# Where the banks of turned attention weights stand between the projections of the next batch

## The chip, the cores and the metric

The kernel runs on one core of one Trainium2 chip. The metric is the device time of one launch in microseconds (us), as the median of several runs. The kernel before takes 2846.47 us (median of three runs, 2845.55 to 2849.2).

## What is computed

The reference is a two-layer block on x of 16 batches x 100 rows x 512 channels, with a context of 16 x 722 x 384, all in fp32. Each layer adds a gated cross-attention to x and then a gated feed-forward network (a mixture of experts in layer 0, a quantized network in layer 1):

```
q = LN(x) @ Wq (+ bq);  k = ctx @ Wk (+ bk);  v = ctx @ Wv (+ bv)
p = softmax(q k^T * D**-0.5)            # over 722 keys, per head
x = x + tanh(g) * ((p v) @ Wo + bo)     # layer 0: 16 heads of 32, layer 1: 8 heads of 64, no bq, bk, bv
x = x + tanh(g_ffn) * ffn(LN(x))
```

The change is in the attention that both layers share.

## The kernel before

**Steps.** The attention goes by 64 steps, (b, m): a batch b and a block m of 128 channels, which holds G = 4 heads in layer 0 and G = 2 in layer 1. TensorE's instructions run in the order in which the program writes them (`manual_schedule` for PE); the other engines' order is set when the program is built, each by a plan of when its operands will be ready, and each then works through its list in that order. `run` (L489 on) writes the order. In the step for (b, m) it issues

- `scores` of the next step (L369): eight short matmuls into two tiles of two PSUM banks each (pool `s`, two tiles). VectorE copies each head's scores out, negated, with a running minimum (L379 and L392; L402 joins the two halves in layer 0) into one of four `ns` tiles. In layer 0 a call covers half of the keys, so a step has two calls; in layer 1 one call covers all;
- `attend` of the step before (L458): 24 products in layer 0 and 12 in layer 1 (two matmul records each) of values and turned weights, chunk by chunk of 128 keys; L465 (VectorE) multiplies the result by the reciprocal of the sums and writes it to `tT`;
- `turn` of this step: ScalarE's exponentials (`softmax`, L411) lie as 100 rows x 722 keys per head, and attend needs keys on partitions. For each pair of heads there are twelve transpositions (L434) into three PSUM banks of four, which ScalarE (L447) or VectorE (L449) copies to a tile `pT`; which of the two is set by whether m + pair + bank is odd. The last bank of the last pair has a fifth transposition (L442) of the reciprocals `rinv`, which VectorE makes with L429 from the sums that the exponentials leave;
- `softmax` of the next step: one exponential per head.

**Units.** Between these stand units of other work, one call each: a bank of the next batch's keys (`keys`, L207, six matmul records, copied by ScalarE at L219 or L221) or values (`values`, L232 and L239), a bank of queries (L329 and L338), of the output projection (`project`, L476 and L483), of a turned tile of x (L131 and L132), of router logits (L627 and L630), or work without TensorE such as moments. Keys and values come at 3.5 units per step, the rest at steps given by hand; the two lists are joined to `units`, the second kind first.

**Banks.** All of these but `scores` take their PSUM bank from one pool of four (tag "mm"), in order; a claim waits until the copy out of the bank that was claimed four claims before has ended. `pT` has three buffers.

**The cut.** With two pairs per step (layer 0), of n units (2n+4)//5 go ahead of pair 0's three banks, up to (3n+4)//5 behind them, then the second call of scores, pair 1's three banks, and the rest. With one pair (layer 1), (n+1)//2 units stand ahead of the three banks and the rest behind.

Of the kernel before, what the change touches and what calls it, by code (L numbers as in the profile page):

```python
# [8 lines left out]
F32 = mybir.dt.float32  # L9
# [7 lines left out]
P = 128  # L17
B, T, C = 16, 100, 512
# [7 lines left out]
NS = -(-S // P)  # L26
# [23 lines left out]
def bcast(ap, *shape):  # L50
    return ap.to_broadcast(list(shape))
# [6 lines left out]
def tiles_for(b):  # L58

    return [i for i in range(NTT) if (i * P + rows_of(i) - 1) // T == b]  # L60
# [74 lines left out]
class Attention:  # L135
# [281 lines left out]
                accum_out=self.sums[b][:, h : h + 1],  # L417
            )

    def turn(self, b, m, pair):  # L420


        nc, D, G = self.net.nc, self.D, self.G
        last = pair == G // 2 - 1
        t = self.p3.tile([P, 2 * NS + 1, T], F32, tag="pT", name="pT")
        if last:
            rinv = self.p2.tile([T, G, D], F32, tag="rinv", name="rinv")
            sums = self.sums[b][:, m * G : (m + 1) * G]
            nc.vector.reciprocal(rinv, bcast(sums.unsqueeze(2), T, G, D))  # L429
        for q in range(3):  # L430
            ps = self.ps_m.tile([P, 5, T], F32, tag="mm", name="ps_t")
            for i in range(4):
                j, c = divmod(4 * q + i, NS)
                nc.tensor.transpose(  # L434
                    ps[:, i, :],
                    self.prob(b, m * G + 2 * pair + j)[:, c * P : (c + 1) * P],
                    self.net.ident[:T, :T],
                )
            n = 4
            if last and q == 2:  # L440
                n = 5
                nc.tensor.transpose(  # L442
                    ps[:, 4, :], rinv.rearrange("p g d -> p (g d)"), self.net.ident[:T, :T]
                )
            to = t[:, 4 * q : 4 * q + n, :]
            if (m + pair + q) % 2:
                nc.scalar.copy(to, ps[:, :n, :])  # L447
            else:
                nc.vector.tensor_copy(to, ps[:, :n, :])  # L449
        self.pT[b, m, pair] = t  # L450

    def attend(self, b, m):
        nc, D, G = self.net.nc, self.D, self.G
# [35 lines left out]
    def run(self, given, after_project=None, more=()):  # L489

        parts = 2 if self.G == 4 else 1
        steps = [(b, m) for b in range(B) for m in range(KC)]
        last_tile = lambda g: ((g + 1) * GT - 1) // P
        extra = {i: [] for i in range(len(steps) + 40)}
        for at, *unit in more:
            extra[at].append(tuple(unit))
        for g in range(1, B // GB):
            at = 4 * KC * (g - 1)  # L500
            for n, i in enumerate(range(last_tile(g - 1) + 1, last_tile(g) + 1)):
                extra[at + 2 + n].append((self.query_input, i))
            for m in range(KC):
                extra[at + 7 + 2 * m].append((self.queries, g, m))
        for b in range(B):
            for i in tiles_for(b):
                at = (b + 1) * KC + 1
                extra[at].append((self.project, i))
                for later, *unit in after_project(i) if after_project else ():
                    extra[at + later].append(tuple(unit))  # L510
        todo = [u for b in range(1, B) for u in self.keys_and_values(b)]
        for i, (b, m) in enumerate(steps):
            if m == 0 and b + 2 < B and b + 2 not in self.cxs:
                self.load_ctx(b + 2)

            upto = max(0, min(len(todo), int(3.5 * (i + 1) - 2)))
            units = extra[i] + todo[given:upto]
            given = max(given, upto)
            nxt = steps[i + 1] if i + 1 < len(steps) else None
            if nxt:  # L520
                self.scores(*nxt, 0)
            if i:
                self.attend(*steps[i - 1])
            n = len(units)
            cut = [0, (n + 1) // 2, n] if parts == 1 else [0, (2 * n + 4) // 5, (3 * n + 4) // 5, n]
            for f, *a in units[cut[0] : cut[1]]:
                f(*a)
            self.turn(b, m, 0)
            for f, *a in units[cut[1] : cut[2]]:
                f(*a)  # L530
            if parts == 2:
                if nxt:
                    self.scores(*nxt, 1)
                self.turn(b, m, 1)
                for f, *a in units[cut[2] :]:
                    f(*a)
            if nxt:
                self.softmax(*nxt)
        self.attend(*steps[-1])
        for i in range(len(steps), len(steps) + 40):  # L540
            for f, *a in extra[i]:
                f(*a)
# [390 lines left out]
def quantized_ffn(net, p, gate, out):  # L933
# [3 lines left out]
    with ExitStack() as ctx:  # L937
# [129 lines left out]
        with tc.manual_schedule(engines={PE}):  # L1067
            for k in range(KC):
                turn(0, FG[0], k)
            for i in range(1, F1 // FT):  # L1070
                weights(i)
            for g, tiles in enumerate(FG):
                between = {}
                if g + 1 < len(FG):
                    normal(FG[g + 1])
                    for k in range(KC):
                        between[NF - 6 + k] = [(turn, g + 1, FG[g + 1], k)]
                feed(g, tiles, between)
# [486 lines left out]
```

## Time and profile before

| what | before |
|---|---|
| median of three runs | 2846.47 us |
| profiled execution, its time | 2848.7 us |
| its span | 2847.0 us |
| granted clock, mean | 0.99 |
| stretch 60 to 930 us, layer 0's attention: TensorE / VectorE / ScalarE busy | 863.8 / 438.8 / 431.0 us |
| stretch 1000 to 1650 us, most of the experts: TensorE busy | 644.2 us |
| stretch 1760 to 2460 us, layer 1's attention: TensorE / VectorE / ScalarE busy | 697.6 / 240.6 / 249.2 us |

The profile is of one execution; its span is the time from the first to the last instruction, and its time is that of the launch. A row of the timeline names the start, the length, the engine, the line of the kernel, the operation, what it writes and reads with the buffer numbers left out, how many records are merged, and, in brackets, how long the engine had been idle and what ended that. PE is TensorE's matmul, PEld its load of weights, DVE is VectorE, ACT is ScalarE, POOL is GpSimd. A matmul's end is modelled and longer than the distance to the next matmul, so lateness on TensorE is read from the distance between starts.

### The profile page before, as it was taken

The numbers are of one execution on the slowest core, as the hardware profiler recorded it, in microseconds if no ns is written. First come the engines' busy times: TensorE is split into PE (matmuls) and PEld (weight loads), VectorE is DVE, ScalarE is ACT, GpSimd is POOL, SyncE is SP. The second block draws the span as 40 slices with busy tenths as digits, with TensorE's granted clock in tenths as the row PEclk, the third lists the DMA queues.
The fourth block names the chain that finished last, engine by engine and source line by source line (L and its number), as shares of the span: only waits on it lengthen the run. The fifth ranks groups of instructions, "written<-read, shape, count | busy, mean of one in ns | idle before, by whom it ended". The sixth has DMA issues, their size and how long they took to land. (4 is left out here: it accounts for less than half of the span.)

```text
span 2847.0 us, 41099 instructions
## 1 busy us (share of the span) xinstructions
PE 2790.3 (98%) x17360; PEld 1732.7 (61%) x17360; DVE 934.0 (33%) x2441; ACT 872.2 (31%) x1726; POOL 168.6 (6%) x187
## 2 busy tenths in 40 slices
PE   8999999999999999999999989999999999799999
PEld 4555555555555678878878845555565555444554
DVE  3544544454455500000000073333333333521100
ACT  2544554454455310000000034333333334211110
POOL 2000000000000000000000050000000000301000
PEclk9999999999999999999999999999999999899999
DMA  4000100000000389898988541000000000430000
GB/s 160 17 17 17 33 24 24 17 28 33 17 24 5 117 329 336 318 318 313 321 313 311 186 130 36 17 16 32 16 17 32 17 32 1 141 96 15 11 12 9
DMA packets 129877, 278.04 MB, mean 98 GB/s; under 512 B 5825, under 2 KB 5841, under 8 KB 129169
## 3 DMA queue, kind: packets, MB, share of 16 engines
q1 hardware_dynamic: 117888, 246.80, 24.9%
q0 software_dynamic: 5088, 16.28, 1.6%
q10 hardware_dynamic: 6704, 12.19, 1.1%
q8 instruction: 141, 2.31, 0.3%
q14 instruction: 56, 0.45, 0.0%
HBM read 260.31 MB, written 14.94 MB: 97 GB/s over the span
## 5 line engine op out<-in xcount | busy, mean ns | idle before, releaser
L232 PE MATMUL ps_v<-wv_a,ctx_a 128*128 128x512 f32 (+1 forms) x1152 | 523.3, 598 | 4.0 <-ACTq L898 1.6
L207 PE MATMUL ps_k<-ctx_a,wk_a 128*128 128x361 f32 x1488 | 488.1, 472 | 0.0
L840 PE MATMUL ps_h<-xT,w 128*128 128x128 f32 x3712 | 421.1, 276 | 4.0 <-DVEq L1450 4.0
L840 PEld LDWEIGHTS ps_h<-xT,w 128*128 128x128 f32 x3712 | 418.6, 193 | 4.7 <-issue 4.7
L207 PEld LDWEIGHTS ps_k<-ctx_a,wk_a 128*128 128x128 f32 x1488 | 271.7, 190 | 150.2 <-issue 12.8
L232 PEld LDWEIGHTS ps_v<-wv_a,ctx_a 128*128 128x128 f32 (+1 forms) x1152 | 204.2, 185 | 238.5 <-issue 227.9
L392 DVE TENSOR_SCALAR_CACHE_REDUCE ns<-ps_s 100x361 f32<-100x361 f32 x512 | 244.5, 525 | 206.8 <-PE ps_s L369 184.9
L434 PEld LDWEIGHTS ps_t<-ident,pr_a 100*128 100x128 f32 x2304 | 215.7, 142 | 83.3 <-issue 43.8
L411 ACT ACTIVATE pr_a<-ns,extremes 100x722 f32<-100x722 f32 x256 | 227.1, 889 | 67.8 <-DVE extremes L402 67.7
L434 PE MATMUL ps_t<-ident,pr_a 100*128 100x100 f32 x2304 | 239.3, 253 | 4.4 <-DVE tT_a L465 4.2
L449 DVE COPY pT<-ps_t 128x400 f32<-128x400 f32 (+1 forms) x288 | 169.6, 593 | 193.4 <-PE ps_t L434 185.5
L369 PE MATMUL ps_s<-kT_a,qT_a 32*100 32x361 f32 (+1 forms) x1536 | 213.9, 502 | 7.4 <-DVE ns L379 4.9
L239 ACT COPY v_a<-ps_v 128x512 f32<-128x512 f32 x192 | 111.3, 579 | 340.1 <-PE ps_v L232 340.1
L860 PE MATMUL ps_o<-w,midT 128*128 128x512 f32 x464 | 203.9, 592 | 0.0
L379 DVE TENSOR_SCALAR_CACHE_REDUCE ns<-ps_s 100x722 f32<-100x722 f32 x128 | 111.3, 907 | 276.1 <-PE ps_s L369 276.1
L447 ACT COPY pT<-ps_t 128x400 f32<-128x400 f32 (+1 forms) x288 | 146.8, 511 | 170.1 <-PE ps_t L434 152.4
L1047 PE MATMUL ps_z<-ffn_w,y_ffn 128*128 128x512 f32 (+1 forms) x416 | 190.8, 594 | 0.0
L1029 PE MATMUL ps_y<-hT,ffn_w 128*128 128x384 f32 (+2 forms) x512 | 183.9, 503 | 0.2 <-DVE hT L1012 0.2
L429 DVE RECIPROCAL rinv<-sums_a 100x128 f32<-100x128 f32 x128 | 121.8, 951 | 184.7 <-ACT pr_a L411 184.7
L458 PEld LDWEIGHTS ps_pv<-pT,v_a 128*32 128x32 f32 (+3 forms) x4608 | 135.2, 120 | 69.0 <-issue 45.8
L851 DVE TENSOR_TENSOR midT<-silu,ps_h 128x512 f32<-128x512 f32 x58 | 39.9, 687 | 389.1 <-PE ps_h L840 389.1
L458 PE MATMUL ps_pv<-pT,v_a 128*32 128x100 f32 (+3 forms) x4608 | 163.1, 254 | 1.1 <-DVE pT L449 0.6
(160 smaller groups left out, 1803.1 us busy)
## 6 DMA issues: line engine op xcount, KB each, us to landing
w<-in_L_ffn_w SPq DMA_DIRECT2D x116, 1024.0 KB, 7.2
w<-in_L_ffn_wo SPq DMA_DIRECT2D x29, 2048.0 KB, 10.2
ctx_a<-in_ctxT SPq DMA_DIRECT2D x30, 1083.0 KB, 5.2
q<-in_L_ffn_fc_q SPq DMA_DIRECT2D x8, 1024.0 KB, 5.3
ffn_w<-in_L_ffn_fc_scales SPq DMA_DIRECT2D x8, 1024.0 KB, 10.8
rows<-ot ACTq DMA_DIRECT2D x29, 256.0 KB, 8.0
xn_d<-xn_moe ACTq DMA_DIRECT2D x12, 256.0 KB, 2.0
ctx_a<-in_ctxT SPq DMA_DIRECT2D x6, 361.0 KB, 5.5
```

What stands on the lines that cost most here:

```text
L207: nc.tensor.matmul(ps, self.wk[:, k, m * P : (m + 1) * P], self.cxs[b][:, k, c * SH : (c + 1) * SH], start=(k == 0), stop=(k == KK - 1),)
L232: nc.tensor.matmul(ps[:n], self.cxs[b][:, k, c * P : c * P + n], self.wv[:, k, :], start=(k == 0), stop=(k == KK - 1),)
L369: nc.tensor.matmul(pss[n // 2][:, n % 2, :SH], self.qT[g][j * D : (j + 1) * D, m, q], self.kT[b, m][j * D : (j + 1) * D, c * SH : (c + 1) ...
L392: nc.vector.tensor_scalar(self.negated[b, m][j][:, part * SH : (part + 1) * SH], pss[j // 2][:, j % 2, :SH], -1.0, BIG, ALU.mult, ALU.min, ...
L411: nc.scalar.activation(self.prob(b, h)[:, :S], ns, AF.Exp, bias=self.nmax[b][:, h : h + 1], scale=-1.0, accum_out=self.sums[b][:, h : h + 1],)
L434: nc.tensor.transpose(ps[:, i, :], self.prob(b, m * G + 2 * pair + j)[:, c * P : (c + 1) * P], self.net.ident[:T, :T],)
L449: nc.vector.tensor_copy(to, ps[:, :n, :])
L458: nc.tensor.matmul(ps[j * D : (j + 1) * D, :], self.v[b][:n, c, m * P + j * D : m * P + (j + 1) * D], self.pT[b, m, j // 2][:n, j % 2 * NS ...
L840: nc.tensor.matmul(ph[:, f, :], w[:, n, k, f * P : (f + 1) * P], self.xT[j][:, k, :], start=(k == 0), stop=(k == KC - 1),)
L860: nc.tensor.matmul(po, self.midT[j, f // 4][:, f % 4, :], w[:, f, :], start=(f == 0), stop=(f == KF - 1),)
L1029: nc.tensor.matmul(ps[:, :nt], w1[f // nf][:, k, f % nf * P : (f % nf + 1) * P], hT[g][:, k, :nt], start=(k == 0), stop=(k == KC - 1),)
L1047: nc.tensor.matmul(z[j][:n], y[:, j * P : j * P + n], w2[f // nf][:, f % nf, :], start=(f == 0), stop=(f == NF - 1),)
```

## The change

`turn` now sets one bank of a pair instead of three, with the bank's number q as an argument; what was done once per pair (the tile `pT`, and the reciprocal in the last pair) is done at q = 0. In `run`, the units of a step are cut evenly over the pairs (halves in layer 0, one part in layer 1), and each part's units are cut in thirds by whole division: a third, bank 0, a third, bank 1, a third, bank 2. With two units in a part the first third is empty; with one unit the first two are. The second call of scores in layer 0 stands between the two parts. Nothing else differs: the same instructions, transfers, tiles and pools.

```diff
--- before.py
+++ after.py
@@ -417,37 +417,35 @@
                 accum_out=self.sums[b][:, h : h + 1],
             )
 
-    def turn(self, b, m, pair):
+    def turn(self, b, m, pair, q):
 
 
         nc, D, G = self.net.nc, self.D, self.G
         last = pair == G // 2 - 1
-        t = self.p3.tile([P, 2 * NS + 1, T], F32, tag="pT", name="pT")
-        if last:
-            rinv = self.p2.tile([T, G, D], F32, tag="rinv", name="rinv")
-            sums = self.sums[b][:, m * G : (m + 1) * G]
-            nc.vector.reciprocal(rinv, bcast(sums.unsqueeze(2), T, G, D))
-        for q in range(3):
-            ps = self.ps_m.tile([P, 5, T], F32, tag="mm", name="ps_t")
-            for i in range(4):
-                j, c = divmod(4 * q + i, NS)
-                nc.tensor.transpose(
-                    ps[:, i, :],
-                    self.prob(b, m * G + 2 * pair + j)[:, c * P : (c + 1) * P],
-                    self.net.ident[:T, :T],
-                )
-            n = 4
-            if last and q == 2:
-                n = 5
-                nc.tensor.transpose(
-                    ps[:, 4, :], rinv.rearrange("p g d -> p (g d)"), self.net.ident[:T, :T]
-                )
-            to = t[:, 4 * q : 4 * q + n, :]
-            if (m + pair + q) % 2:
-                nc.scalar.copy(to, ps[:, :n, :])
-            else:
-                nc.vector.tensor_copy(to, ps[:, :n, :])
-        self.pT[b, m, pair] = t
+        if q == 0:
+            self.pT[b, m, pair] = self.p3.tile([P, 2 * NS + 1, T], F32, tag="pT", name="pT")
+            if last:
+                self.rinv = self.p2.tile([T, G, D], F32, tag="rinv", name="rinv")
+                sums = self.sums[b][:, m * G : (m + 1) * G]
+                nc.vector.reciprocal(self.rinv, bcast(sums.unsqueeze(2), T, G, D))
+        ps = self.ps_m.tile([P, 5, T], F32, tag="mm", name="ps_t")
+        for i in range(4):
+            j, c = divmod(4 * q + i, NS)
+            nc.tensor.transpose(
+                ps[:, i, :],
+                self.prob(b, m * G + 2 * pair + j)[:, c * P : (c + 1) * P],
+                self.net.ident[:T, :T],
+            )
+        n = 4
+        if last and q == 2:
+            n = 5
+            rinv = self.rinv.rearrange("p g d -> p (g d)")
+            nc.tensor.transpose(ps[:, 4, :], rinv, self.net.ident[:T, :T])
+        to = self.pT[b, m, pair][:, 4 * q : 4 * q + n, :]
+        if (m + pair + q) % 2:
+            nc.scalar.copy(to, ps[:, :n, :])
+        else:
+            nc.vector.tensor_copy(to, ps[:, :n, :])
 
     def attend(self, b, m):
         nc, D, G = self.net.nc, self.D, self.G
@@ -521,19 +519,17 @@
                 self.scores(*nxt, 0)
             if i:
                 self.attend(*steps[i - 1])
-            n = len(units)
-            cut = [0, (n + 1) // 2, n] if parts == 1 else [0, (2 * n + 4) // 5, (3 * n + 4) // 5, n]
-            for f, *a in units[cut[0] : cut[1]]:
-                f(*a)
-            self.turn(b, m, 0)
-            for f, *a in units[cut[1] : cut[2]]:
-                f(*a)
-            if parts == 2:
-                if nxt:
-                    self.scores(*nxt, 1)
-                self.turn(b, m, 1)
-                for f, *a in units[cut[2] :]:
-                    f(*a)
+
+            for part in range(parts):
+                if part and nxt:
+                    self.scores(*nxt, part)
+                n = len(units)
+                mine = units[n * part // parts : n * (part + 1) // parts]
+                n = len(mine)
+                for q in range(3):
+                    for f, *a in mine[n * q // 3 : n * (q + 1) // 3]:
+                        f(*a)
+                    self.turn(b, m, part, q)
             if nxt:
                 self.softmax(*nxt)
         self.attend(*steps[-1])
```

## The prediction

> **What bounds the kernel now.** I read the page's first three parts, then the busy time of each engine by stretch, then the start times of the matmul records one by one, then the timeline of single steps.
>
> From the page:
>
> ```profile
> PE 2790.3 (98%) x17360; PEld 1732.7 (61%) x17360; DVE 934.0 (33%) x2441; ACT 872.2 (31%) x1726; POOL 168.6 (6%) x187
> ...
> PEclk9999999999999999999999999999999999899999
> ...
> L434 PE MATMUL ps_t<-ident,pr_a 100*128 100x100 f32 x2304 | 239.3, 253 | 4.4 <-DVE tT_a L465 4.2
> ```
>
> From the stretches (us; busy PE, PEld, DVE, ACT, POOL; granted clock; DMA share; GB/s), layer 0's attention:
>
> ```profile
> 60.00:930.00 870.00, 863.81 (x6975) 502.21 (x6977) 438.81 (x1441) 431.00 (x891) 21.86 (x24) 1.00 0.06 21
> ```
>
> TensorE sets the time of the stage; VectorE and ScalarE are half idle, transfers are nearly nothing. Only what makes TensorE start a matmul late can be won or lost. A busy figure hides this, since a matmul's row is longer than the distance to the next (a transposition's row has 253 ns, the next starts 86 ns later). So I took start-to-start distances. Six matmuls of a key unit take 1.84 us, of a value unit 2.57, a bank of four transpositions 0.34, the fifth 0.09. Between 62 and 930 us, twenty starts in or just after the three banks in a row come later than 86 ns, by 9.23 us together (0.09 to 1.02 each). In layer 1 (1760 to 2445) there is not one over 0.06 us. That is all that spreading can win: 9.2 us, 0.3% of 2847.
>
> One step around such a wait. Columns: start, length, engine, line, operation, count, and in brackets idle time and its end:
>
> ```profile
> 450.46 0.87 PE L369 MATMUL ps_s<-kT_a,qT_a 32*100 32x361 f32 x8
> 451.26 1.25 PE L434 MATMUL ps_t<-ident,pr_a 100*128 100x100 f32 x12
> 452.43 3.83 PE L207 MATMUL ps_k<-ctx_a,wk_a 128*128 128x361 f32 x12
> 453.18 0.57 DVE L449 COPY pT<-ps_t 128x400 f32<-128x400 f32 x1
> 453.67 0.15 DVE L402 TENSOR_TENSOR extremes<-nmh 100x4 f32<-100x4 f32 x1
> 453.85 0.90 ACT L411 ACTIVATE pr_a<-ns,extremes 100x722 f32<-100x722 f32 x1 [1.11 <-DVE extremes L402]
> 455.63 0.54 ACT L219 ACTIVATE kT_a<-ps_k,bkc_a 128x361 f32<-128x361 f32 x1
> 456.19 0.87 PE L369 MATMUL ps_s<-kT_a,qT_a 32*100 32x361 f32 x8
> 456.95 0.89 ACT L411 ACTIVATE pr_a<-ns,extremes 100x722 f32<-100x722 f32 x1
> 456.99 1.24 PE L458 MATMUL ps_pv<-pT,v_a 128*32 128x100 f32 x48
> 457.83 0.54 ACT L219 ACTIVATE kT_a<-ps_k,bkc_a 128x361 f32<-128x361 f32 x1
> 457.96 0.95 DVE L429 RECIPROCAL rinv<-sums_a 100x128 f32<-100x128 f32 x1 [3.56 <-ACT pr_a L411]
> 460.59 0.26 DVE L465 TENSOR_TENSOR tT_a<-ps_pv,pT 128x100 f32<-128x100 f32 x1
> 460.90 0.91 PE L434 MATMUL ps_t<-ident,pr_a 100*128 100x100 f32 x8 [0.85 <-DVE tT_a L465]
> ```
>
> Second half of the scores at 450.46; VectorE copies them; four exponentials run 453.85 to 457.83. The reciprocal (L429) waits for them on VectorE, the next scores' copies queue behind it, then tT (L465, 460.59), which frees attend's bank. Four "mm" banks were taken by then (attend, logits, a turned tile, one bank of weights), so the second bank of weights started 1.02 us late.
>
> **The change, part by part.** Instructions, DMAs and queues are the same; only TensorE's order is rewritten (L524 on), and the other engines follow it.
>
> *Spread banks.* In layer 0 a step's units are now cut in equal halves around the second scores; before, most stood ahead of them. I wrote out both orders for all 128 steps. With two units to a half, it runs bank, unit, bank, unit, bank. For each step I added the times above from the scores to the claim of the fifth "mm" bank, and compared it with L465 (10.1 us after the second scores in the step shown; here 9.8 with the earlier exponentials below). Every late step of before now claims at 9.75 us or later (most over 11), but for the last batch's step with hardly any unit, which keeps 0.6 to 1.5 us. Gain 7.7 to 9.2; I take **-8.5**. What is late next there is nothing but the matmuls.
>
> *First unit after attend.* In 52 places of the stage a key, value, query or output unit loses 65 to 104 ns inside, as the first after attend's small tiles (5.0 us); transpositions after attend or a unit show none. With less than three units in a half a bank now comes first. 13 such places are left, and 29 new ones behind scores, which before never stood ahead of a unit, so 0 to 0.1 us each. Gain 0.9 to 3.8; **-2**.
>
> *The third bank's copy, a new wait.* Before, one to four units and the scores stood between the last bank of a step and the attend that reads it. Now that bank is the step's last work and only 0.8 us of scores covers its copy. Take a half with two key units and m even, whose third bank ScalarE copies. From the second scores: bank until 1.20, keys 3.04, bank 3.38, keys 5.22, five transpositions 5.65, scores at 5.75, attend at 6.55. Attend waits piece by piece, as the last step of layer 1 shows, where nothing stands between:
>
> ```profile
> 2445.77 0.39 PE L458 MATMUL ps_pv<-pT,v_a 128*64 128x100 f32 x2
> 2446.62 0.56 PE L458 MATMUL ps_pv<-pT,v_a 128*64 128x100 f32 x8 [0.47 <-ACT pT L447]
> 2447.77 0.90 PE L458 MATMUL ps_pv<-pT,v_a 128*64 128x100 f32 x14 [0.58 <-DVE pT L449]
> ```
>
> With four heads the third bank is read from record 23 of 48, 21 ns apart: at 7.0. ScalarE: exponentials began at 3.39 in the step above; there a copy of a bank (453.18) stood before the minimum on VectorE, which now comes later, so they begin at 2.90. Four at 0.88 and one copy of keys between (0.44) end at 6.88. Who goes first is fixed when the program is built, by a plan for each engine but TensorE. In the rows keys ready at 3.9 stand behind the second exponential, values ready at 4.7 behind the third, the second keys, ready at 5.7, behind the fourth. A third bank ready at 5.85 will so stand behind the fourth, and behind the second keys' copy: 6.88 + 0.44 + 0.58 = 7.9. Attend loses 0.95. Behind attend in TensorE's queue is the whole next step.
>
> Twelve steps are of this form: 11.4. Eleven with keys and values reach record 23 at 7.75, the copy ends at 7.95: 0.25 each, 2.7 (ready and due both move by 0.7, the fourth exponential does not). In three odd steps with two value units VectorE copies, and the reciprocal, planned before it, holds it until 8.8: 9.5 against 8.45, 3.3 together. Three key units, or four units: the block is over; two key units in an odd step: the copy is planned before the reciprocal; nothing. Sum **+17.4**. Below: 0, if the copy goes ahead of the fourth exponential. Above: if the exponentials still begin at 3.39, 0.49 more in 23 steps, 28.7. I take 17.4, nearest to the orders seen.
>
> *Layer 1.* One half per step; scores take 1.39, its two exponentials end 4.3 us after they begin, far ahead of the last bank, whose copy (0.6) is covered. There were no late starts to win: 0.
>
> Sum -8.5 - 2 + 17.4 = **+7**. On the profiled execution (span 2847.0, time 2848.7) that is 2855.6; on the median shown, 2846.47, it is 2853.4, and I give 2853.
>
> The clock was 1.00 in the stage with its twenty late starts, so the new ones, up to 1.1 us each, cost me only their length. The Trainium skill speaks against that: TensorE: Matmul & The Clock Gate, "A second HAM failure mode: psum-queue depth-cycling", says that short idle times between groups, from cycling through banks, can make the clock fall and rise. By its 3.4 us window at half speed ("What's actually happening"), an estimate of 1.7 us for each of 26 waits would add 44 us; by the row it adds 0.
>
> **Rivals.**
> - *The copy goes ahead* (other side: faster). If the plan puts the third bank before the fourth exponential, ScalarE ends it by 7.0 to 7.5 and attend loses at most a few tenths. The point is record 23 at 7.0. Then -8.5 - 2 + 3 = -7.5: 2839. For it: ScalarE is half idle. Against it: three kinds of copies in the rows stand the other way.
> - *Half and half.* Short waits of 0.4 us in the twelve steps, the others as above: +10.8 - 10.5, near 0: 2847.
> - *More waits.* The exponentials don't begin earlier, or the reciprocal overtakes the copy in the 13 other odd steps with two or three key units (1 us each): 24 to 30 instead of 17: 2862.
> - *It does not spread.* With one unit in a half two banks still stand in a row, with none three; 23 of 128 halves of layer 0 are such. That costs 1 to 3 us of the gain and lies in the forecast's range.
>
> **How the numbers follow.** Forecast 0.4, the copy ahead 0.2, half and half 0.2, more waits 0.2. The bounds of the terms give -9.2 - 3.8 + 0 = -13 to -7.7 - 0.9 + 28.7 = +20: 2833 to 2867. Cutting the lower end, where all three terms would have to be at their best, leaves 2838 to 2866. A difference under 0.2% (5.7 us) can't be told from none: the forecast lies just over it, in 3 of its 4 tenths slower and in one within; half and half is within; more waits slower; the copy ahead faster. Faster 0.2, same 0.3, slower 0.5.
>
> **What would show it.** The late starts at L434 and after them gone from layer 0. In the waits view, L458 waiting for pT of L447, some twenty times, 0.2 to 1 us, in even steps. In the timeline of a half with two key units: four exponentials, a copy of keys, then the copy of 128x500 after attend has begun. First exponential 2.9 after the scores in even steps. Layer 1's stretch unchanged to 1 us. Wrong if L458 waits for nothing (then it is faster), if L465 still frees banks late, or if the granted clock falls below 1.00 in the stage.

## The result, and the profile after

The changed kernel takes 2875.82 us (median of six runs, 2873.7 to 2878.34) against 2847.45 us for the kernel before (median of six, 2845.55 to 2849.46): a ratio of 1.01, with a 95% interval of 1.0087 to 1.0113. It is slower by 1%. The profiled execution took 2874.8 us with a span of 2873.1, which is 26.1 us more than the span before. The prediction had the direction and the mechanism, and too small a size.

In the changed kernel the helper's lines have moved a little: the bank's copies are L446 (ScalarE) and L448 (VectorE), the reciprocal L430, its transposition L443, attend L456, and the product that frees attend's bank L463.

From the page of the profile after, the lines that answer to those of before, and attend's group:

```profile
PE 2802.5 (98%) x17360; PEld 1754.1 (61%) x17360; DVE 940.5 (33%) x2441; ACT 857.1 (30%) x1726; POOL 169.8 (6%) x187
...
PEclk9999999999999999999999989999999999899999
...
L434 PE MATMUL ps_t<-ident,pr_a 100*128 100x100 f32 x2304 | 293.1, 254 | 0.4 <-ACT pr_a L411 0.4
...
L456 PE MATMUL ps_pv<-pT,v_a 128*32 128x100 f32 (+3 forms) x4608 | 175.4, 254 | 19.3 <-ACT pT L446 10.6
```

The idle time ahead of the transpositions has gone (4.4 us before, 0.4 now). In its place 19.3 us stand ahead of attend, most of it put down to a copy of turned weights by ScalarE. From the waits view of TensorE between 60 and 955 us (total, times, longest):

```profile
PE ps_pv L456 <- ACT pT L446: 9.2, 11, 1.2
PE ps_pv L456 <- DVE pT L448: 5.7, 12, 0.8
```

From the stretches (us; busy PE, PEld, DVE, ACT, POOL; granted clock; DMA share; GB/s), layer 0's attention with and without its first 15 us:

```profile
60.00:930.00 870.00, 854.53 (x6781) 503.62 (x6781) 432.57 (x1396) 407.57 (x869) 21.94 (x24) 0.99 0.06 21
75.00:930.00 855.00, 839.86 (x6681) 495.17 (x6679) 424.05 (x1367) 398.71 (x848) 21.94 (x24) 1.00 0.06 21
```

In the same 870 us TensorE gets through 6781 matmul records where it had 6975, and VectorE and ScalarE are still half idle. From 75 us on the clock was 1.00. In the 15 us ahead of that it was 0.66, where it had been 0.85 before; that stretch lies ahead of the stage that the account below takes.

One half of a step with two key units and m even, the form for which the prediction worked out its wait (start, length, engine):

```profile
94.72 0.87 PE L369 MATMUL ps_s<-kT_a,qT_a 32*100 32x361 f32 x8
...
97.76 0.90 ACT L411 ACTIVATE pr_a<-ns,extremes 100x722 f32<-100x722 f32 x1 [1.09 <-DVE extremes L402]
...
100.30 0.25 PE L443 MATMUL ps_t<-ident,rinv 100*128 100x100 f32 x1
...
100.86 0.89 ACT L411 ACTIVATE pr_a<-ns,extremes 100x722 f32<-100x722 f32 x1
101.28 0.72 PE L456 MATMUL ps_pv<-pT,v_a 128*32 128x100 f32 x22
101.74 0.55 ACT L219 ACTIVATE kT_a<-ps_k,bkc_a 128x361 f32<-128x361 f32 x1
...
102.18 0.56 ACT L446 COPY pT<-ps_t 128x500 f32<-128x500 f32 x1
...
102.80 0.88 PE L456 MATMUL ps_pv<-pT,v_a 128*32 128x100 f32 x26 [0.81 <-ACT pT L446]
```

The third bank is whole at 100.55. ScalarE takes it at 102.18, after its fourth exponential and a copy of keys. Attend stops after record 22, at the place and behind the two instructions that the prediction named. The next record would have followed 21 ns after the 22nd; by the distance of starts it is 1.03 us late, while the bracket says 0.81, since a matmul's row is longer than the distance to the next.

The account, from distances between matmul starts beyond what their columns take. The stage from the first to the 59th attend of layer 0 took 837.0 us before and 856.5 after:

| | before | after | predicted change | measured change |
|---|---|---|---|---|
| late starts at and after the rows of banks | 8.2 | 0 | -8.5 | -8.2 |
| late records inside attend | 0 | 22.2 in 33 attends | +17.4 | +22.2 |
| all other distances inside attend | 57.6 | 61.7 | 0 | +4.1 |
| first matmuls after another kind, and the rest | | | -2 | +1.3 |
| from the 59th attend to the 64th, the last of layer 0 | 46.1 | 50.4 | in the terms above | +4.2 |
| up to the first attend | | | 0 | +1.3 |
| layer 1's attention | | | 0 | +1.8 |

That adds up to 26.7 us; the span grew by 26.1, and the 0.6 are spread over the rest.

The row up to the first attend goes with the clock and is not shown to be an effect of the change. In ten of the eleven profiles of this case a stretch at half clock begins between 57.6 and 60.9 us, and the first attend comes later the longer that stretch is: at 68.4 us in the one profile without it, at 70.3 to 71.5 in the four with 6.8 us of it (before is one of them), and at 71.8 to 73.1 in the six with 10.2 us of it (the changed kernel is one of them).

### The profile page after: what moved, and what is told of

Read it like the earlier page. It is cut to its first block, busy times and chain, and to the rows that moved or that the text cites. A ratio compares the mean times of both kernels' runs of the same rounds, so it can differ in the third digit from the quotient of the medians.

```text
span 2873.1 us, 41126 instructions
## 1 busy us (share of the span) xinstructions
PE 2802.5 (98%) x17360; PEld 1754.1 (61%) x17360; DVE 940.5 (33%) x2441; ACT 857.1 (30%) x1726; POOL 169.8 (6%) x187
## 5 line engine op out<-in xcount | busy, mean ns | idle before, releaser
L207 PE MATMUL ps_k<-ctx_a,wk_a 128*128 128x361 f32 x1488 | 495.9, 473 | 0.8 <-DVE tT_a L463 0.8
L434 PEld LDWEIGHTS ps_t<-ident,pr_a 100*128 100x128 f32 x2304 | 251.1, 143 | 179.8 <-issue 124.8
L207 PEld LDWEIGHTS ps_k<-ctx_a,wk_a 128*128 128x128 f32 x1488 | 265.7, 190 | 133.9 <-issue 6.8
L434 PE MATMUL ps_t<-ident,pr_a 100*128 100x100 f32 x2304 | 293.1, 254 | 0.4 <-ACT pr_a L411 0.4
L448 DVE COPY pT<-ps_t 128x400 f32<-128x400 f32 (+1 forms) x288 | 169.2, 589 | 353.3 <-PE ps_t L434 189.2
L392 DVE TENSOR_SCALAR_CACHE_REDUCE ns<-ps_s 100x361 f32<-100x361 f32 x512 | 241.5, 527 | 72.1 <-PE ps_s L369 68.4
L446 ACT COPY pT<-ps_t 128x400 f32<-128x400 f32 (+1 forms) x288 | 146.5, 509 | 283.3 <-PE ps_t L434 278.0
L430 DVE RECIPROCAL rinv<-sums_a 100x128 f32<-100x128 f32 x128 | 121.9, 952 | 235.3 <-ACT pr_a L411 235.3
L456 PEld LDWEIGHTS ps_pv<-pT,v_a 128*32 128x32 f32 (+3 forms) x4608 | 139.5, 119 | 95.2 <-issue 47.3
L456 PE MATMUL ps_pv<-pT,v_a 128*32 128x100 f32 (+3 forms) x4608 | 175.4, 254 | 19.3 <-ACT pT L446 10.6
```

Source lines behind the costliest of these rows:

```text
L207: nc.tensor.matmul(ps, self.wk[:, k, m * P : (m + 1) * P], self.cxs[b][:, k, c * SH : (c + 1) * SH], start=(k == 0), stop=(k == KK - 1),)
L392: nc.vector.tensor_scalar(self.negated[b, m][j][:, part * SH : (part + 1) * SH], pss[j // 2][:, j % 2, :SH], -1.0, BIG, ALU.mult, ALU.min, ...
L434: nc.tensor.transpose(ps[:, i, :], self.prob(b, m * G + 2 * pair + j)[:, c * P : (c + 1) * P], self.net.ident[:T, :T],)
L456: nc.tensor.matmul(ps[j * D : (j + 1) * D, :], self.v[b][:n, c, m * P + j * D : m * P + (j + 1) * D], self.pT[b, m, j // 2][:n, j % 2 * NS ...
```

## The experiments

Three theories stood at the start. The first is the prediction's: the third bank of the second pair is the step's last work, and its copy stands behind the exponentials (or, on VectorE, behind the reciprocal) in an in-order queue. The second has two forms: the even cut of the units costs by itself (theory 2 of the expectations), or tearing the rows apart does, since TensorE then changes more often between kinds of matmul (the rival of the third experiment). The third: the step's chain from scores over exponentials to L463 is too long for an even cut, and the wait will turn up elsewhere when the third bank is moved. All ratios are to the kernel before, with a 95% interval. "Stage" is the time from the first to the 59th attend.

**Bank first, then its units.** From the changed kernel:

```diff
                 for q in range(3):
+                    self.turn(b, m, part, q)
                     for f, *a in mine[n * q // 3 : n * (q + 1) // 3]:
                         f(*a)
-                    self.turn(b, m, part, q)
```

> The changed kernel with one thing turned round in both layers: in each third the bank stands first and the third's units behind it, so that the last units of a part stand between its third bank and the next scores and attend. The spread, the even cut and every instruction stay. Theory 1 (the third bank's copy, behind the exponentials on ScalarE or the reciprocal on VectorE, makes attend wait): attend's inner late starts, 22 us between the first attend and the 59th in the changed kernel, fall to under 2 us, the late starts after the banks stay under 3 us, and the time is 2838 to 2846 us, 0 to 9 under before. Theory 2 (the even cut of the units around the second scores costs by itself): still 15 us or more above before, 2862 to 2876. Theory 3 (the wait only moves: without it the bank that L463 frees comes late instead): attend's waits gone, but 10 to 20 us of late starts at the banks or the units after them, 2855 to 2868.

Measured: 2863.66 us, 1.0059 (1.0045 to 1.0072); stage 846.4. Attend waits for nothing, and the other distances inside it are back at 57.6. But about half of the loss returned at another place. The step after three key units:

```profile
114.82 1.24 PE L456 MATMUL ps_pv<-pT,v_a 128*32 128x100 f32 x48
...
117.45 0.26 DVE L463 TENSOR_TENSOR tT_a<-ps_pv,pT 128x100 f32<-128x100 f32 x1
...
117.77 0.48 PE L434 MATMUL ps_t<-ident,pr_a 100*128 100x100 f32 x3 [0.44 <-DVE tT_a L463]
```

Attend runs through; now banks follow directly behind it, four "mm" banks are soon taken, and the fifth claim waits for L463, which VectorE reaches only after the reciprocal and the copies of the next scores. The waits view has 15.0 us of it in 16 places. The time lies in the ranges of the second and the third theory; the places of the waits speak for the third. What follows: the waits at attend are due to where the third bank stands (first theory), and the third theory holds for this order.

**The third bank on VectorE in every step.**

```diff
-        if (m + pair + q) % 2:
+        if (m + pair + q) % 2 and not (G == 4 and last and q == 2):
```

> The changed kernel, but in layer 0 the third bank of the second pair is always copied by VectorE; before, ScalarE copied it in even steps. Nothing is moved on TensorE. Theory 1: in the 23 even steps with two units in the second part attend's wait goes (12 of 1.03 us and 11 of 0.31 us inside, with what follows each wait 17 to 19 us in all), in odd steps it stays (9 of 0.6, 3 of 0.9, about 9 us): 2856 to 2860 us. Theory 2 (the even cut): no change, 2873 to 2878. Theory 3 (the wait only moves): attend's waits gone in even steps and as much lateness elsewhere, 2870 to 2876.

Measured: 2870.94 us, 1.0075 (1.0062 to 1.0088); stage 855.2. In even halves with two key units the wait went from 1.03 us to none. In even halves with keys and values it rose from 0.31 to 0.90, because on VectorE the copy is planned behind the reciprocal; three steps then also waited for L463 (3.6 us). So the expectation was too good: the engine is not what matters, the place in its queue is. The time lies in the third theory's range, but only these 3.6 us are of its kind. Odd halves stayed as they were (0.64 and 0.95).

**The row of three banks behind the half's units.**

```diff
+                for f, *a in mine:
+                    f(*a)
                 for q in range(3):
-                    for f, *a in mine[n * q // 3 : n * (q + 1) // 3]:
-                        f(*a)
                     self.turn(b, m, part, q)
```

> The even cut of the changed kernel, but three banks in a row again, behind all units of a part. Theory 1: the third bank is as late as in the changed kernel, and the first and second are now late too, so attend waits in at least the same 35 steps, and longer in some: 2876 to 2890 us. A rival (tearing the row of banks apart is what costs): no separate banks, so back to 2847 to 2852.

Measured: 2869.08 us, 1.0067 (1.0054 to 1.008); stage 855.7. The row is whole again and most of the loss stays, so tearing it apart is not the main cause. The first theory's size was too high here: attend waits in more places for less (13.7 us at 48 records, 8.6 more than before in its other distances, 6.5 more at its first record). The longest of these waits stand mostly at its fifth record, the first that reads this row.

**The row ahead of the half's units.**

```diff
                 for q in range(3):
-                    for f, *a in mine[n * q // 3 : n * (q + 1) // 3]:
-                        f(*a)
                     self.turn(b, m, part, q)
+                for f, *a in mine:
+                    f(*a)
```

> The even cut of the changed kernel, but three banks in a row ahead of all units of a part. Theory 1: attend never waits for a copy (under 2 us in all), but attend and three banks now take the four banks within 2.2 us, and the next unit or bank waits for the one that L463 frees: about 16 steps by 1.2 us and 11 by 0.5, 20 to 28 us: 2860 to 2872. That is what the spread is worth under this cut. Theory 2 (the even cut costs by itself, whatever stands where): 2870 to 2876, without long late starts at one place. If the bank from L463 does not matter: 2840 to 2847.

Measured: 2888.61 us, 1.0136 (1.0121 to 1.015); stage 864.7. No wait at attend, and 33.7 us in 28 places where the first unit behind the first pair's row waits for L463, 1.7 us each after two key units. The place is the expected one, the size larger. Here attend and the three banks of the next row take four claims at once, so the unit behind them claims the fifth, and L463 has not yet come. After one of these waits the clock fell, the only time between the first and the 59th attend in any profile of this case (first the unit's row, then the stretch with its granted clock of 0.51):

```profile
780.68 3.57 PE L207 MATMUL ps_k<-ctx_a,wk_a 128*128 128x361 f32 x6 [1.50 <-DVE tT_a L463]
...
781.10:784.50 3.40, 3.40 (x10) 1.61 (x12) 0.49 (x2) 0.22 (x1) 0.00 (x0) 0.51 0.00 0
```

The matmuls of this unit start 0.60 us apart instead of 0.30; by the starts that cost 1.7 us beside the wait.

**The first pair spread, the second pair's row directly behind the scores.** The even cut stays.

```diff
                 for q in range(3):
-                    for f, *a in mine[n * q // 3 : n * (q + 1) // 3]:
-                        f(*a)
+                    if not part:
+                        for f, *a in mine[n * q // 3 : n * (q + 1) // 3]:
+                            f(*a)
                     self.turn(b, m, part, q)
+                for f, *a in mine if part else ():
+                    f(*a)
```

> The changed kernel, but the second pair of layer 0 again sets its three banks in a row, right after the second scores, with its units behind; the first pair (and layer 1) stay spread, and the cut stays even. Theory 1, as it now stands (two waits: attend for a third bank's copy, and a late claim of the bank that L463 frees some 10 us after the second scores): attend waits for nothing; L463 at 10 to 10.2 us after the scores; the fifth claim of a step comes before it in 3 steps with a turned tile of x ahead of keys (about 1.1 us each) and hardly elsewhere, so late starts of 3 to 6 us: 2843 to 2852. Theory 2 (the even cut costs by itself): 2855 or more. If the spread of the first pair is what makes banks late: 10 to 20 us of late starts, 2852 to 2866.

Measured: 2850.71 us, 1.0006 (0.9997 to 1.0015); stage 833.3. The whole loss is gone. So the even cut and the spread of the first pair together cost no more than they gain, and the second theory falls in the form with the even cut; what is left is the second pair's spread. Three late units remain (1.53 us each, for L463). The stage is 3.7 us shorter than before; layer 1, which has the change, gives 1.5 of them back (see the layer 1 run below), and the first attend starts 1.8 us later, with the clock.

**Shorter exponentials in layer 0**, with TensorE's order of the changed kernel:

```diff
-            nc.gpsimd.memset(t[:, S:], 0.0)
+            nc.gpsimd.memset(t[:, SH if self.G == 4 else S :], 0.0)
...
-                self.prob(b, h)[:, :S],
-                ns,
+                self.prob(b, h)[:, : SH if G == 4 else S],
+                ns[:, : SH if G == 4 else S],
```

> The changed kernel with layer 0's exponentials over 361 of 722 keys (the other half of the weights is zero, so the output is not the reference's): each exponential is about 0.3 us shorter, four of them 1.2 us. Order on TensorE unchanged. Theory 1: the copies behind them come 1.2 us earlier, so the waits of 1.03, 0.31 and 0.6 us inside attend vanish or nearly so; with the changed kernel's small rest the time falls by 18 to 27 us, to 2849 to 2858. Theory 2 (the even cut, or the order itself on TensorE, costs whatever ScalarE does): 2870 to 2876.

Measured: 2841.84 us, 0.9977 (0.9968 to 0.9986); stage 829.2. The end of the same half as shown above:

```profile
96.53 0.59 ACT L411 ACTIVATE pr_a<-ns,extremes 100x361 f32<-100x361 f32 x1
...
97.56 0.56 ACT L446 COPY pT<-ps_t 128x500 f32<-128x500 f32 x1
97.86 1.24 PE L456 MATMUL ps_pv<-pT,v_a 128*32 128x100 f32 x48
```

Each exponential takes 0.59 us instead of 0.88; the copy begins 6.3 us after the second scores instead of 7.5, ends before its record is due, and attend's 48 records run through. TensorE's order alone makes no wait when ScalarE's queue is short, which is the first theory's strongest test. It need not be free: the stage is 3.4 us longer than in the last experiment below, which has no such waits either and keeps its rows whole; how much of that is the torn rows and how much the cut is not shown. The time fell below the expectation, and below the kernel before, since the late starts at the rows are gone as well.

**Layer 1 alone changed.** Layer 0 has the order of before:

```diff
+            if parts == 2:
+                for f, *a in units[cut[0] : cut[1]]:
...
+            else:
+                for q in range(3):
+                    for f, *a in units[n * q // 3 : n * (q + 1) // 3]:
+                        f(*a)
+                    self.turn(b, m, 0, q)
```

> The change in layer 1 alone; layer 0 in the order of before. All theories that put the loss into layer 0: 2847 to 2851, the start-to-start account of layer 1 in the changed kernel having 1 to 2 us more than before. If layer 1 holds part of the loss that the account does not show: 2853 or more.

Measured: 2849.34 us, 1.0005 (0.9996 to 1.0015). By the time this can't be told from no change; by the profile layer 1 is about 2.0 us longer, and the span 2.2. The one long wait is of the kind of layer 0: at the third attend of layer 1, VectorE comes to the third bank only after the last sums of the experts (L929), and attend stops after record 10, for 1.5 us by its starts:

```profile
1707.61 0.66 DVE L448 COPY pT<-ps_t 128x500 f32<-128x500 f32 x1
...
1708.32 0.90 PE L456 MATMUL ps_pv<-pT,v_a 128*64 128x100 f32 x14 [1.28 <-DVE pT L448]
```

Over the other steps layer 1 falls behind by some 0.02 us each.

**The second pair alone spread**, from the kernel before: the old cut, the first pair's row, and layer 1 stay.

```diff
-                self.turn(b, m, 1)
-                for f, *a in units[cut[2] :]:
+                mine = units[cut[2] :]
+                n = len(mine)
+                for q in range(3):
+                    for f, *a in mine[n * q // 3 : n * (q + 1) // 3]:
+                        f(*a)
+                    self.turn(b, m, 1, q)
```

> The kernel before with one part of the change alone: in layer 0 the units behind the second scores are set in thirds between the second pair's banks, third bank last. The old cut, the first pair's row and layer 1 stay as before. Theory 1 (the third bank's copy stands behind exponentials or the reciprocal): with one unit the third bank ends 3.9 us after the scores and attend reads it at 5.2; in even steps ScalarE copies it behind two exponentials and perhaps the keys, to 5.2 to 6.1, so waits of 0 to 0.9 us in some 25 steps; in odd steps VectorE is free, no wait with one unit, and with two units as in the changed kernel. The late starts at the first pair's row, 8 to 9 us, stay or shrink. Together 4 to 22 us over before: 2853 to 2870. If the even cut is needed for the loss: 2846 to 2851.

Measured: 2880.73 us, 1.0112 (1.0095 to 1.0129); stage 868.7. A half with one key unit:

```profile
94.99 0.25 PE L443 MATMUL ps_t<-ident,rinv 100*128 100x100 f32 x1
...
96.87 0.56 ACT L446 COPY pT<-ps_t 128x500 f32<-128x500 f32 x1
...
97.48 0.72 PE L456 MATMUL ps_pv<-pT,v_a 128*32 128x100 f32 x24 [0.81 <-ACT pT L446]
```

The bank is whole at 95.24 and copied 1.63 us later; attend is 1.03 us late by its starts, as in the changed kernel. In all, 26.6 us in 36 attends, and 4.5 in their other distances; the first pair's late starts stay (8.1 us). It lost more than expected: some two dozen halves wait about 1 us (those with one or two key units in even steps, and eight with two value units in odd ones). This one edit makes the whole loss, and without the even cut it is larger than in the changed kernel.

**The units between the first row and the second scores put ahead of that row**, from the kernel before, all rows kept whole:

```diff
             cut = [0, (n + 1) // 2, n] if parts == 1 else [0, (2 * n + 4) // 5, (3 * n + 4) // 5, n]
+            if parts == 2:
+                cut[1] = cut[2]
```

> The kernel before (three banks in a row), with one edit in layer 0: the units that stood between the first pair's row and the second scores stand ahead of that row. Theory 1: the fifth claim of a step moves 1.8 to 2.6 us later, past L463's copy, in all steps that had late starts at the row but the last batch's; attend still waits for nothing, as the second pair's row stays right behind the scores: 7 to 9 us of late starts go, 2838 to 2842 us. If the six banks now nearly in a row wait for each other's copies: late starts at the second pair's row, 2846 to 2860.

Measured: 2837.09 us, 0.9962 (0.9948 to 0.9975); stage 825.8. It beats both kernels. The step shown of before in the prediction, now:

```profile
455.72 1.99 PE L207 MATMUL ps_k<-ctx_a,wk_a 128*128 128x361 f32 x6
...
456.77 0.26 DVE L465 TENSOR_TENSOR tT_a<-ps_pv,pT 128x100 f32<-128x100 f32 x1
...
457.54 1.20 PE L434 MATMUL ps_t<-ident,pr_a 100*128 100x100 f32 x12
```

One more unit stands ahead of the row, so L465 has freed attend's bank before the row claims it, and twelve transpositions run at 86 ns. All 8.2 us of late starts are gone, attend waits for nothing; the other 3.0 us of the 11.2 in this stage are smaller distances between matmuls. The late starts go by moving units, without taking a row apart.

## Why the prediction fell short

Its direction was right, and in even steps so were its mechanism and its place: the third bank's copy behind the fourth exponential and the second keys' copy, a wait after record 22 of attend. The step that failed is the size of "the third bank's copy, a new wait": +17.4 against 22.2 in this stage, 2.5 in the last batch's two halves of the form, and 4.1 around the waits. The largest part of the miss, 5.7 us, comes from a form of odd step for which it put the wait at nothing.

- *Spread banks, -8.5:* right (-8.2). L463 came 9.8 us after the second scores in the step shown, as assumed, and no bank claims before it.
- *Halves with two key units, m even, 0.95 each:* 1.03 in ten, and 1.13 and 1.38 in the last batch. Together 12.8 instead of 11.4. The first exponential began 3.04 us after the scores, not 2.90; the copy ended at 8.0, not 7.9.
- *Keys and values, m even, 0.25 each:* 0.31 in eleven; 3.4 instead of 2.7. *Two value units, m odd, 3.3 together:* 0.94 in three, 2.8.
- *Three key units, m odd, "the block is over":* wrong, 0.63 in nine, 5.7 instead of 0. The odd half's queues, from the timeline of one whose second scores began at 107.17:

```profile
113.81 0.48 ACT L446 COPY pT<-ps_t 128x400 f32<-128x400 f32 x1
...
114.18 0.91 ACT L411 ACTIVATE pr_a<-ns,extremes 100x722 f32<-100x722 f32 x1
...
115.21 0.95 DVE L430 RECIPROCAL rinv<-sums_a 100x128 f32<-100x128 f32 x1 [4.20 <-ACT pr_a L411]
...
116.08 0.62 DVE L448 COPY pT<-ps_t 128x500 f32<-128x500 f32 x1
...
116.75 0.47 PE L456 MATMUL ps_pv<-pT,v_a 128*32 128x100 f32 x12 [0.44 <-DVE pT L448]
```

  The second bank's copy and two copies of keys were planned ahead of the fourth exponential, which so began 7.0 us after the scores; the reciprocal waited for it until 8.0 and the third bank's copy, planned behind it, until 8.9. I had moved the copies in ScalarE's list and left the exponentials where they were without them. This is the rival *more waits* in part: in nine of its thirteen steps, by 0.63 instead of 1 us; the four odd halves with two key units didn't wait. All other forms waited for nothing, as predicted.
- *Nothing after a wait:* wrong, 4.1 us. The records behind a late one lose another 0.12 us per attend.
- *First unit after attend, -2:* wrong, +1.3 with the rest. The prediction read that a transposition behind attend loses nothing, and that was wrong: its second start comes 142 ns after the first instead of 86, in the three such places of the trace of before too. Units did lose less behind attend (2.7 us), but 37 more transpositions there lose 56 ns each (2.0 us). Behind scores, 29 units lose 66 or 104 ns each (2.9 us), and 29 transpositions fewer there lose 1.6 less. Some forty more key units behind a bank of transpositions lose 26 ns each (1.3 us with a few longer ones).
- *Layer 1 and the start, 0:* +1.8 and +1.3. The layer 1 edit alone shows 2.0, with the one long wait shown there, which the prediction had as covered. The start goes with the clock, as said under the account.
- *Last batch:* +4.2, of which 2.5 are its two halves of the form above; the other 1.7 weren't traced.

From +7 to +26.1 are 19.1 us. With the last batch's two waits counted with their form they are 7.3 for the wait term (24.7 instead of 17.4), 4.1 for what follows a wait, 3.3 for first units, 0.3 for the spread, and 1.7 + 1.3 + 1.8 for what was counted at nothing: 19.8, and -0.7 in the rest.

*The clock.* It stayed at 1.00 from 75 to 930 us with 33 waits of up to 1.0 us, so these waits cost their length and what is said above, not a slower clock. The rule of the Trainium skill that the prediction weighed (TensorE: Matmul & The Clock Gate, "A second HAM failure mode: psum-queue depth-cycling") would have added 44 us by the estimate there; this run shows none of it. Longer waits are not shown to be harmless: with the row ahead of the half's units, one of 28 waits, of 1.7 us, was followed by 3.4 us at half clock, which cost 1.7 us, as much as the estimate put on every wait.

Another page of the Trainium skill, Perfetto Trace Analysis ("Optimization Strategy"), says that the same gap repeating on the engine that should be busy can mean too little room in SBUF or PSUM for the next tile. At the rows of before that agrees: the claim waited for a bank, 8.2 us in the stage. At the changed kernel's attend it does not lead on: the bank was claimed and full, and in the half shown waited 1.6 us for its turn in the copying engine's queue. No run here adds a bank.

## What to carry to other kernels

Put a PSUM bank's work where the engine that copies it out is free, not where TensorE has room: here the gap of some 3 us between the scores and the first exponential took three copies for nothing, and a third bank some 4 us later made attend wait 0.3 to 1.0 us in 33 of 58 steps. Count from a bank's last matmul to its reader against the whole in-order list of the copying engine, with every copy that is newly planned ahead; an engine that is half idle on average says nothing about that. If a row waits for a bank, try first to move other work ahead of it.

## What was not expected of the hardware

After a wait inside attend's run of small products (128x100 by 32 columns, 21 ns apart) the records behind the late one lose more: 4.1 us over 33 attends in the changed kernel and 4.5 over 36 with the second pair alone spread, some 0.12 us each, and none (57.6 us as before) in every kernel without such waits. The profile's waits understate this kind of loss: 23 waits of 14.9 us in that view between 60 and 955 us, where the starts show 33 attends and 22.2 us in a shorter stretch.
